# An involution's first block made of the image's edge rows, so that taps outside of the image are left out

## The chip, the cores and the metric

The kernel runs on one core of a Trainium2 chip. The metric is the device time of one launch in microseconds (us): the median of 3 runs for the kernel before. A core has a matrix engine (PE, or TensorE), which multiplies a stationary block of weights with a moving block and adds into PSUM; three elementwise engines, DVE (VectorE), ACT (ScalarE) and POOL (GpSimd); and SP, which here only issues DMA transfers. The engines run side by side and wait for each other through semaphores; each takes its own instructions in the order of the program.

## What is computed

The input `x` is 32 images of 256 channels and 32x32 pixels. Two residual layers follow each other; the change touches only the second, an *involution*: a 7x7 window over each pixel, with a window of weights that is computed for every pixel and shared by the 16 channels of each of 16 groups.

```python
# layer 0: x = x + conv3x3(groupnorm(x)), operands and result rounded to a 16-bit format, plus bias
x = x + L0(gn(x))
# layer 1, on v = gn(x):
y   = relu(bn(w1 @ v))                     # 256 -> 64 channels, 1x1
w   = (w2 @ y + b2).reshape(b, 16, 49, 32, 32)   # 49 weights per group and pixel
vp  = pad(v, 3 on each side)               # zeros outside of the image
out[b, g, c, h, j] = sum over (di, dj) in 7x7 of  w[b, g, (di,dj), h, j] * vp[b, g, c, h+di, j+dj]
x = x + out
```

`vp` is zero outside of the image. For the output row 0, the three taps `di` = 0, 1, 2 therefore give nothing; row 1 has two such taps and row 2 has one, and the same holds at the bottom for rows 31, 30 and 29. That is 12 of 32 x 7 = 224 pairs of a row and a vertical tap.

## The kernel before

An image is worked on in `NB` = 4 blocks of `BR` = 8 rows. A block takes four *stages*: the horizontal taps are split in two parts `v` (4 taps `dj`, then 3; one tap per 32 partitions, so 128 or 96 partitions), and the vertical taps in two parts `d` (`di` 0 to 3, then 4 to 6). An image has 16 stages, numbered here 0 to 15 in the order (k, v, d). A stage has two parts:

- `products`: weights times pixels, elementwise. DVE takes the first rows of the block, straight from PSUM; POOL takes the last rows, from an SBUF copy `ws` of the weights.
- `sums`: PE adds the products of all partitions into the 8 rows of the block. The stationary operand `shift` is a 0/1 matrix with 32 columns that moves a pixel by its `dj`. It fills only 32 of the array's 128 columns, so four such products stand side by side in four *column tiles*: tile `t` makes output rows 2t and 2t+1 (2 rows x 256 channels = 512 moving columns).

```python
COLS = (tuple(range(0, 4)), tuple(range(4, 7)))      # dj of v = 0 and 1
DI = ((0, 4), (4, 7))                                # di of d = 0 and 1
POOL_ROWS = (4, 6)                                   # POOL's first row, for d = 0 and 1

def load_pixels(b, i):                               # SBUF copy of the pixels, i = upper or lower half
    first = PAD1 if i == 0 else 0                    # 3 rows of zeros above, 16+3 rows of the image
    rows = XR - PAD1                                 # 19
    for r0, r1 in ((0, BR + PAD1), (BR + PAD1, rows)):
        for q in range(Q):                           # once per 32 partitions
            nc.sync.dma_start(xpix[i][q * W : (q + 1) * W, first + r0 : first + r1], ...)

def weights(b, k, v):                                # all 7 di at once, into PSUM
    for r in range(BR):
        for q, dj in enumerate(COLS[v]):
            nc.tensor.matmul(pw[q * W : (q + 1) * W, ...], y_pad[b % 2][:, k * BR + r, ...], w2_sb[:, dj, :], ...)
    nc.scalar.copy(ws[:p], pw[:p, 1, ...])           # rows 4 to 7, for POOL

def products(b, k, v, d, pw, ws):
    d0, d1 = DI[d]
    for r0, nr in ((0, 4), (4, 2), (6, 2)):
        on_pool = r0 >= (6 if (k, v) == (NB - 1, 1) else POOL_ROWS[d])
        tag, bufs = ("pg", 4) if on_pool else ("pa", 2) if nr == 4 else ("pb", 2)
        pt = prodp.tile([P, nr, d1 - d0, C], F32, tag=tag, name=tag, bufs=bufs)
        eng.tensor_tensor(o, win.unsqueeze(3).to_broadcast([p, nr, n, GC]), xin, ALU.mult)
        # ... prods[t] = the two rows of tile t

def sums(acc, v, d, prods):
    for i in range(d0, d1):
        for t in range(T):
            nc.tensor.matmul(acc[t * W : (t + 1) * W, :], shift[v][:p], prods[t][:p, :, i - d0, :], ...)

def finish(b, k, acc):                               # in three steps
    nc.scalar.copy(ob, acc...)                       # 1
    yield
    ... four nc.tensor.transpose(po[...], ob[...], ident)      # 2
    yield
    nc.vector.tensor_tensor(xt[:, :, cols], po..., xt[:, :, cols], ALU.add)   # 3: one add for 8 rows
    if k % 2 == 1:
        nc.sync.dma_start(out..., xt[:, :, cols])    # 16 rows

for n in range(FRONT, len(stages) + 3):              # one step per stage (cut to the order of issue)
    now = stages[n], products(*stages[n], *pws[n // 2])
    sums(acc, v, d, prods)                           # of stage n - 1
    next(ending, None)                               # a step of finish
    if n % 2 == 0:
        pws[n // 2 + 1] = weights(*stages[n + 2][:3])
    ... # one piece of the front of a later image
```

A *step* is one turn of this loop. In step n, DVE and POOL get the products of stage n, and PE gets the sums of stage n-1, on even steps the weights of stage n+2, and a piece of the *front* of a later image: group norm, the 3x3 convolution (`pc`, 18 matmuls for each of 4 units), the second group norm, the transposes `pt` and the product `py`. In step 0 the front has ACT apply the first group norm (`xq`), which the convolution's matmuls of step 1 read. In steps 1, 5, 9 and 13, POOL has an add (`x<-qb,x`) that waits for a convolution unit to have passed PE, DVE and ACT.

Of the kernel before, what the change touches and what calls it, by code (L numbers as in the profile page):

```python
# [9 lines left out]
F32 = mybir.dt.float32  # L10
AF = mybir.ActivationFunctionType
ALU = mybir.AluOpType

P = 128
B, C, H, W = 32, 256, 32, 32
N = H * W
NT = 512
RT = NT // W
CH = C // P
K0, PAD0 = 3, 1  # L20
H0 = H + 2 * PAD0
K1, PAD1 = 7, 3
TAPS = K1 * K1
CR = 64
G = 16
GC = C // G
# [7 lines left out]
Q = 4  # L34
COLS = (tuple(range(0, 4)), tuple(range(4, 7)))
DI = ((0, 4), (4, 7))
BR = 8
NB = H // BR
T = 4
HALF = H // 2  # L40
POOL_ROWS = (4, 6)
HOLD = 6
FRONT = -38
LOAD = -42
XR = HALF + 2 * PAD1


@with_exitstack
def tile_quant_conv_then_involution(
# [15 lines left out]
    nc = tc.nc  # L65
# [33 lines left out]
    pixels = {}  # L99
# [5 lines left out]
    for base, mult, step in ((0, 1, -GN), (GN - 1, -1, GN)):  # L105
        nc.gpsimd.affine_select(
            out=avg_g,
# [10 lines left out]
    shift = []  # L118
    for v, cols in enumerate(COLS):
        s = const.tile([P, W], F32, name=f"shift_{v}")  # L120
        nc.gpsimd.memset(s, 0.0)
        for q, dj in enumerate(cols):
            rows = s[q * W : (q + 1) * W]
            nc.gpsimd.affine_select(
                out=rows,
# [14 lines left out]
    nc.gpsimd.memset(three_halves, 1.5)  # L140

    xpix = [const.tile([P, XR, C], F32, name=f"xpix_{i}") for i in range(2)]
    nc.gpsimd.memset(xpix[0][:, :PAD1], 0.0)
    nc.gpsimd.memset(xpix[1][:, XR - PAD1 :], 0.0)
    y_pad = [const.tile([CR + 1, H, W + 2 * PAD1], F32, name=f"y_{i}") for i in range(2)]
    for t in y_pad:
        nc.gpsimd.memset(t[:CR], 0.0)
# [28 lines left out]
    prodp = ctx.enter_context(tc.tile_pool(name="prodp", bufs=2))  # L176
# [70 lines left out]
    def front(b):  # L247
# [65 lines left out]
        for r in range(0, H // 4, 2):  # L313
# [8 lines left out]
            for i in range(4):  # L322
                nc.sync.dma_start(xd[:, 4 * r + i : 4 * r + i + 5 : 4, :], xt4[i * W : (i + 1) * W])
            yield
        load_pixels(b, 0)

        py = ps_m.tile([P, NT], F32, tag="m", name="py")
# [18 lines left out]

    def load_pixels(b, i):

        first = PAD1 if i == 0 else 0
        rows = XR - PAD1  # L350
        for r0, r1 in ((0, BR + PAD1), (BR + PAD1, rows)):
            for q in range(Q):
                nc.sync.dma_start(
                    xpix[i][q * W : (q + 1) * W, first + r0 : first + r1],
                    pixels[b][:, i * (H - rows) + r0 : i * (H - rows) + r1, :],
                )

    def weights(b, k, v):


        pw = ps_w.tile([P, 2, NT], F32, tag="pw", name="pw")
        for r in range(BR):
            for q, dj in enumerate(COLS[v]):
                s = 2 * PAD1 - dj
                o = (r % 4) * K1 * G
                nc.tensor.matmul(  # L366
                    pw[q * W : (q + 1) * W, r // 4, o : o + K1 * G],
                    y_pad[b % 2][:, k * BR + r, s : s + W],
                    w2_sb[:, dj, :],
                    start=True,  # L370
                    stop=True,
                )
        p = W * len(COLS[v])
        ws = work.tile([P, 4, K1 * G], F32, tag="ws", name="ws")
        nc.scalar.copy(ws[:p], pw[:p, 1, : 4 * K1 * G].rearrange("p (r m) -> p r m", r=4))  # L375
        return pw, ws

    def products(b, k, v, d, pw, ws):

        d0, d1 = DI[d]  # L380
        p = W * len(COLS[v])
        n = (d1 - d0) * G
        half, first = divmod(k * BR, HALF)
        src = xpix[half]
        prods = {}
        for r0, nr in ((0, 4), (4, 2), (6, 2)):
            xin = bass.AP(
                tensor=src.tensor,
                offset=src[:p, first + r0 + d0, 0:1].offset,
                ap=[src[:p].ap[0], [C, nr], [GC, n], [1, GC]],  # L390
            )
            on_pool = r0 >= (6 if (k, v) == (NB - 1, 1) else POOL_ROWS[d])
            if on_pool:
                win = ws[:p, r0 - 4 : r0 - 4 + nr, d0 * G : d1 * G]
            else:
                o = (r0 % 4) * K1 * G
                win = pw[:p, r0 // 4, o : o + nr * K1 * G].rearrange("p (r m) -> p r m", r=nr)
                win = win[:, :, d0 * G : d1 * G]
            tag, bufs = ("pg", 4) if on_pool else ("pa", 2) if nr == 4 else ("pb", 2)
            pt = prodp.tile([P, nr, d1 - d0, C], F32, tag=tag, name=tag, bufs=bufs)  # L400
            o = pt[:p].rearrange("p r d (g c) -> p r (d g) c", c=GC)
            eng = nc.gpsimd if on_pool else nc.vector
            eng.tensor_tensor(o, win.unsqueeze(3).to_broadcast([p, nr, n, GC]), xin, ALU.mult)  # L403
            for t in range(r0 // 2, (r0 + nr) // 2):
                prods[t] = pt[:, 2 * t - r0 : 2 * t - r0 + 2]
        return prods

    def sums(acc, v, d, prods):
        d0, d1 = DI[d]
        p = W * len(COLS[v])  # L410
        for i in range(d0, d1):
            for t in range(T):
                nc.tensor.matmul(  # L413
                    acc[t * W : (t + 1) * W, :],
                    shift[v][:p],
                    prods[t][:p, :, i - d0, :],
                    start=v == 0 and i == 0,
                    stop=v == len(COLS) - 1 and i == K1 - 1,
                )

    def finish(b, k, acc):

        ob = work.tile([P, 2, C], F32, tag="ob", name="ob", bufs=1)
        nc.scalar.copy(ob, acc.rearrange("p (r c) -> p r c", c=C))  # L424
        yield
        po = acc.rearrange("p (h t r j) -> p h t r j", h=CH, t=T, r=2)
        for h in range(CH):
            for r in range(2):
                nc.tensor.transpose(po[:, h, :, r, :], ob[:, r, h * P : (h + 1) * P], ident)  # L429
        yield  # L430
        xt = x_tiles[b]
        cols = slice(k * BR * W, (k + 1) * BR * W)
        nc.vector.tensor_tensor(
            xt[:, :, cols], po.rearrange("p h t r j -> p h (t r j)"), xt[:, :, cols], ALU.add
        )
        if k % 2 == 1:
            cols = slice((k - 1) * BR * W, (k + 1) * BR * W)
            nc.sync.dma_start(out[b].rearrange("(h p) n -> p h n", p=P)[:, :, cols], xt[:, :, cols])
        if k == NB - 1:
            x_tiles.pop(b)  # L440
        yield
# [3 lines left out]
    stages = [  # L445
        (b, k, v, d) for b in range(B) for k in range(NB) for v in range(len(COLS)) for d in range(len(DI))
    ]
    per = len(stages) // B
    with tc.manual_schedule():
        fronts, done = {}, {}  # L450
        ending = iter(())
        acc = last = None
        pws = {}
        for n in range(FRONT, len(stages) + 3):
            if 0 <= n < len(stages):
                b, k, v, d = stages[n]
                now = stages[n], products(b, k, v, d, *pws[n // 2])
            else:
                now = None
            if last is not None:  # L460
                (b, k, v, d), prods = last
                if (v, d) == (0, 0):
                    acc = ps_acc.tile([P, NT], F32, tag="acc", name="acc")
                sums(acc, v, d, prods)
            next(ending, None)
            if last is not None and (v, d) == (len(COLS) - 1, len(DI) - 1):
                ending = finish(b, k, acc)
                next(ending)
            last = now
            b, at = divmod(n, per)  # L470
            if at == 0 and 0 <= b < B:
                load_pixels(b, 1)
            if 0 <= n + 2 < len(stages) and n % 2 == 0:
                pws.pop(n // 2 - 1, None)
                pws[n // 2 + 1] = weights(*stages[n + 2][:3])
            b, at = divmod(n - LOAD, per)
            if at == 0 and 0 < b < B:
                x_tiles[b] = load_x(b)
            b, at = divmod(n - FRONT, per)
# [48 lines left out]
```

## Time and profile before

| | before |
|---|---|
| time, median of 3 (lowest to highest) | 2862.68 us (2862.51 to 2863.04) |
| span of the profiled execution | 2862.9 us, granted PE clock 0.994 of full speed |
| busy: PE, DVE, POOL, ACT | 98%, 92%, 92%, 37% |
| DMA: mean share of the 16 engines, mean rate | 37.5% for all queues, 93 GB/s |
| matmul records on the sums' line | 14336 (7168 calls, two records each) |
| from the same point of one image to the next, in the middle of the run | 86.82 us (1483.47 to 1570.29) |

A profile row names the engine, the operation, the output and the inputs with their shapes (partitions x elements), and gives busy time, mean duration of one, and idle time before. Busy times of overlapping matmuls are not sums of their durations: four column tiles at work count once. The chain of waits is the list of work that, followed back from the last instruction, set the end: its pieces add up to the time.

### The profile page before, as it was taken

To read this page: it belongs to the slowest core of one execution; us is meant where nothing else is said; L and a number is where in the kernel's file an instruction comes from. 1 tells how busy PE (TensorE), PEld (TensorE's weight loads), DVE (VectorE), ACT (ScalarE), POOL (GpSimd) and SP (SyncE) were. 2 spreads that over 40 slices of the span, in tenths; PEclk is the share of its full clock that TensorE was granted. 3 is DMA by queue.
4 is the path that set the end of the run, shared out by engine and by line. 5 is a ranking of instruction groups with operands and counts; after the bars stand their busy time and mean duration, and the time that the engine had idled before them with its cause. 6 is when DMAs were issued, how large, how long until landed. Compare 5 with 4: busy or idle time off the path is not lost.

```text
span 2862.9 us, 73387 instructions
## 1 busy us (share of the span) xinstructions
PE 2805.4 (98%) x32576; PEld 1216.1 (42%) x32576; DVE 2621.2 (92%) x1131; ACT 1047.9 (37%) x2179; POOL 2639.3 (92%) x891
## 2 busy tenths in 40 slices
PE   5999999999999999999999999999999999999998
PEld 2444444444444444444444444444444444444443
DVE  1799999999999999999999999999999999999998
ACT  5443333333343433343433333333433333434210
POOL 2899999999999999999999999999999999999997
PEclk8999999999999999999999999999999999999999
DMA  2444433344433344332444333444333444323440
GB/s 94 98 105 114 93 81 98 83 108 101 101 87 83 97 109 93 97 98 72 106 111 94 83 98 82 107 104 101 84 87 94 108 93 100 95 73 90 97 101 16
DMA packets 93709, 267.45 MB, mean 93 GB/s; under 512 B 19341, under 2 KB 52109, under 8 KB 76750
## 3 DMA queue, kind: packets, MB, share of 16 engines
q1 hardware_dynamic: 93390, 262.75, 36.8%
q8 instruction: 254, 4.16, 0.6%
q14 instruction: 65, 0.53, 0.1%
HBM read 195.57 MB, written 67.11 MB: 92 GB/s over the span
## 4 chain that ended last, share of the span: by engine, by line
PE 91%; ACT 5%; issue 1%; POOL 1%; DVE 1%; DMA 1%; SPq 0%; ACTq 0%; POOLq 0%; DVEq 0%
PE acc L413 52%; PE pc L280 18%; PE pw L366 13%; PE pt L317 2%; PE py L330 2%; PE acc L429 2%; PE pg L196 1%; ACT xq L236 1%; POOL pg L403 1%; ACT qb L296 1%; ACT w L227 1%; DMA xpix<-xd 1%; DVE pb L403 1%; DVE pa L403 0%; ACT off L235 0%
## 5 line engine op out<-in xcount | busy, mean ns | idle before, releaser
L403 POOL TENSOR_TENSOR pg<-ws,xpix 128x2048 f32<-128x2048 f32 (+3 forms) x736 | 2469.2, 3387 | 69.5 <-ACT ws L375 52.7
L403 DVE TENSOR_TENSOR pa<-pw,xpix 128x4096 f32<-128x4096 f32 (+3 forms) x512 | 1987.1, 3882 | 162.2 <-ACT junk L188 87.2
L413 PE MATMUL acc<-pg,shift 128*32 128x512 f32 (+1 forms) x5376 | 1646.2, 596 | 1.4 <-POOL pg L403 1.3
L413 PE MATMUL acc<-pa,shift 128*32 128x512 f32 (+1 forms) x7168 | 1641.9, 596 | 2.6 <-DVE pa L403 2.4
L413 PE MATMUL acc<-pb,shift 96*32 96x512 f32 (+1 forms) x1792 | 825.9, 598 | 5.0 <-DVE pb L403 5.0
L413 PEld LDWEIGHTS acc<-pa,shift 128*32 128x32 f32 (+1 forms) x7168 | 374.2, 109 | 843.9 <-issue 792.7
L280 PE MATMUL pc<-xq,wq 128*128 128x512 f16 x2304 | 577.1, 387 | 18.6 <-ACT xq L236 15.3
L403 DVE TENSOR_TENSOR pb<-pw,xpix 128x1536 f32<-128x1536 f32 (+2 forms) x288 | 519.5, 1804 | 0.0
L366 PEld LDWEIGHTS pw<-w_sb,y 65*32 65x32 f32 x14336 | 414.2, 110 | 151.6 <-issue 150.5
L366 PE MATMUL pw<-w_sb,y 65*32 65x112 f32 x14336 | 446.0, 260 | 0.0
L375 ACT COPY ws<-pw 128x448 f32<-128x448 f32 (+1 forms) x256 | 135.8, 530 | 756.3 <-PE pw L366 750.3
L413 PEld LDWEIGHTS acc<-pg,shift 128*32 128x32 f32 (+1 forms) x5376 | 377.2, 109 | 64.8 <-issue 56.3
L280 PEld LDWEIGHTS <-wq 128*128 128x128 f16 x2304 | 213.5, 99 | 311.3 <-issue 120.1
L298 POOL TENSOR_TENSOR x<-qb,x 128x512 f32<-128x512 f32 x128 | 164.7, 1286 | 136.6 <-ACT qb L296 125.5
L424 ACT COPY ob<-acc 128x512 f32<-128x512 f32 x128 | 75.1, 587 | 481.8 <-PE acc L413 480.5
L413 PEld LDWEIGHTS acc<-pb,shift 96*32 96x32 f32 (+1 forms) x1792 | 174.1, 110 | 33.4 <-issue 18.0
L321 ACT COPY xt<-pt 128x512 f32<-128x512 f32 x128 | 75.0, 586 | 228.6 <-PE pt L317 127.4
L188 ACT ACTIVATE junk<-x 128x512 f16<-128x512 f32 (+1 forms) x192 | 148.0, 771 | 10.7 <-POOL x L298 6.1
L188 ACT ACTIVATE junk<-x,mean 128x1024 f16<-128x1024 f32 x128 | 147.2, 1150 | 4.1
L294 DVE TENSOR_SCALAR q<-pc 128x512 f16<-128x512 f32 x128 | 86.9, 679 | 31.6 <-PE pc L280 31.6
L429 PEld LDWEIGHTS acc<-ident,ob 128*128 128x128 f32 x512 | 53.6, 140 | 108.1 <-issue 82.2
L296 ACT ACTIVATE qb<-q,bias_sb 128x512 f32<-128x512 f16 x128 | 92.5, 722 | 12.0 <-DVE q L294 11.9
(52 smaller groups left out, 971.0 us busy)
## 6 DMA issues: line engine op xcount, KB each, us to landing
xpix<-xd SPq DMA_DIRECT2D x256, 352.0 KB, 6.5
xpix<-xd SPq DMA_DIRECT2D x256, 256.0 KB, 8.6
x<-in_x SPq DMA_DIRECT2D x64, 512.0 KB, 3.7
xd<-xt SPq DMA_DIRECT2D x512, 64.0 KB, 1.7
out<-x SPq DMA_DIRECT2D x64, 512.0 KB, 3.2
wf<-in_w SPq DMA_DIRECT2D x2, 1152.0 KB, 8.7
w_sb<-in_w SPq DMA_DIRECT2D x1, 199.1 KB
w_sb<-in_w SPq DMA_DIRECT2D x1, 64.0 KB, 9.7
```

Of the source, the lines that this page charges most:

```text
L188: nc.scalar.activation(junk[:, n0:n1], src[:, h, n0:n1], func, bias=bias, accum_out=self.sums[:, part, h : h + 1])
L280: nc.tensor.matmul(pc, wq[:, kh, k, mh * P : (mh + 1) * P], xq[:, kh, nt * RT + i0 : nt * RT + i0 + RT, j0 : j0 + W], start=n == 0, stop=n ...
L294: nc.vector.tensor_scalar(q, pc, F16_MAX, -F16_MAX, ALU.min, ALU.max)
L296: nc.scalar.activation(qb, q, AF.Identity, bias=bias_sb[:, mh : mh + 1])
L298: nc.gpsimd.tensor_tensor(xt[:, mh, cols], qb, xt[:, mh, cols], ALU.add)
L321: nc.scalar.copy(xt4, pt)
L366: nc.tensor.matmul(pw[q * W : (q + 1) * W, r // 4, o : o + K1 * G], y_pad[b % 2][:, k * BR + r, s : s + W], w2_sb[:, dj, :], start=True, s ...
L375: nc.scalar.copy(ws[:p], pw[:p, 1, : 4 * K1 * G].rearrange("p (r m) -> p r m", r=4))
L403: eng.tensor_tensor(o, win.unsqueeze(3).to_broadcast([p, nr, n, GC]), xin, ALU.mult)
L413: nc.tensor.matmul(acc[t * W : (t + 1) * W, :], shift[v][:p], prods[t][:p, :, i - d0, :], start=v == 0 and i == 0, stop=v == len(COLS) - 1 ...
L424: nc.scalar.copy(ob, acc.rearrange("p (r c) -> p r c", c=C))
L429: nc.tensor.transpose(po[:, h, :, r, :], ob[:, r, h * P : (h + 1) * P], ident)
```

## The change

Block 0 is no longer rows 0 to 7. It is rows 0 to 3 and 28 to 31; the other three blocks are rows 4 to 11, 12 to 19 and 20 to 27. All rows with taps outside of the image are then in one block, and in this block those products and sums are not made. The four column tiles of PE run side by side, so a tile gains time only if all four lose the same work; hence the pairs. Tile 0 takes rows 0 and 3 (3 + 0 taps outside), tile 1 rows 1 and 2 (2 + 1), tile 2 rows 28 and 31, and tile 3 rows 29 and 30: each pair leaves out 3 of 14.

In block 0, one stage of each `v` is "full": `di` 3 to 6 for the four upper rows and `di` 0 to 3 for the four lower rows, all inside of the image. The other is the "corner" stage: what is left, which is 6 row-taps at the top and 6 at the bottom, all made on DVE in six small instructions, and summed with matmuls of one row (256 columns) or two rows (512). Full and corner come in the order full, corner (v = 0), corner, full (v = 1).

```diff
+EDGE = BR // 2
+ROWS = [[*range(EDGE), *range(H - EDGE, H)]] + [
+    [*range(k * BR - EDGE, (k + 1) * BR - EDGE)] for k in range(1, NB)
+]
+HELD = ([*range(15), *range(25, H)], [*range(9, H - 1)])      # image rows in the two pixel buffers
-XR = HALF + 2 * PAD1
+XR = len(HELD[0])                                             # 22 rows, as before
-    nc.gpsimd.memset(xpix[0][:, :PAD1], 0.0)                  # rows of zeros are no longer needed
-    nc.gpsimd.memset(xpix[1][:, XR - PAD1 :], 0.0)
 def load_pixels(b, i):
-        for r0, r1 in ((0, BR + PAD1), (BR + PAD1, rows)):
+        for r0, r1 in (((0, 7), (15, 22), (7, 15)), ((0, 14), (14, 22)))[i]:
 def weights(b, k, v):
-                    y_pad[b % 2][:, k * BR + r, s : s + W],
+                    y_pad[b % 2][:, ROWS[k][r], s : s + W],
+    CORNERS = (                     # (column of pt, rows) to sum; (row, first di, last di + 1, where) to make
+        ([(0, 1), (1, 1), (2, 1)], [(3, 0, 3, slice(0, 3))]),
+        ([(3, 1), (4, 2)], [(2, 1, 3, slice(3, 6, 2)), (1, 2, 3, slice(4, 5))]),
+        ([(6, 0), (7, 0), (8, 0)], [(4, 4, 7, slice(6, 9))]),
+        ([(9, 2), (11, 0)], [(5, 4, 6, slice(9, 12, 2)), (6, 4, 5, slice(10, 11))]),
+    )
 def products(b, k, v, d, pw, ws):
+        if k == 0 and d == v:                                  # full
+            multiply(k, v, pw, ws, top, 0, 1, 4, 3, 7, False)  # DVE: 4 rows, di 3..6
+            for t in range(2, T):                              # POOL: rows 4 and 7, then 5 and 6, di 0..3
+                multiply(k, v, pw, ws, pt, 2 + t, 7 - 2 * t, 2, 0, 4, True)
+        elif k == 0:                                           # corner
+            for t, (moved, made) in enumerate(CORNERS):
+                for r, d0, d1, at in made:
+                    multiply(k, v, pw, ws, pt[:, at], r, 1, 1, d0, d1, False)
+        else:
-            on_pool = r0 >= (6 if (k, v) == (NB - 1, 1) else POOL_ROWS[d])
+                on_pool = r0 >= POOL_ROWS[d]
 def sums(acc, v, d, moves):
+        for i in range(most):
             for t in range(T):
+                if i < len(moves[t]):
+                    moving, of = moves[t][i]                   # of: 2 for both rows, else the row
+                    cols = slice(0, NT) if of == 2 else slice(of * C, (of + 1) * C)
+                    nc.tensor.matmul(acc[t * W : (t + 1) * W, cols], shift[v][:p], moving, ...)
 def finish(b, k, acc):
+        if k == 0:                                             # four adds of two rows, for the scattered rows
+            for t in range(2):
+                for r in range(2):
+                    nc.vector.tensor_tensor(at, po[:, :, t : t + 3 : 2, r], at, ALU.add)
-        if k % 2 == 1:                                         # out: 16 and 16 rows
+        for when, r0, r1 in ((NB - 2, 0, H - EDGE - BR), (NB - 1, H - EDGE - BR, H)):   # out: 20 and 12 rows
```

(Cut: the helper `multiply`, which holds the former body of `products`, the offsets of the rows in the pixel buffers, and the unchanged parts.)

Three things come along with the skipped taps. The two pixel buffers hold 22 rows of the image each, where they held 19 and 3 rows of zeros, so more is loaded. The exception by which DVE took more of stage 14 (k = 3, v = 1, d = 0: six rows in place of four) is gone, so POOL makes four rows there as in the other stages with d = 0. And the output leaves in 20 and 12 rows.

More of the change, by code (lines that the diff above doesn't have):

```diff
@@ L39 @@
 T = 4
-HALF = H // 2
+EDGE = BR // 2
[3 more added lines that the diff above has]
+HELD = ([*range(15), *range(25, H)], [*range(9, H - 1)])
+BASE = ((-PAD1, 15 - EDGE), (1, 1), (0, 0), (8, 8))
 POOL_ROWS = (4, 6)
@@ L347, in load_pixels @@
     def load_pixels(b, i):
-        first = PAD1 if i == 0 else 0
-        rows = XR - PAD1
-        for r0, r1 in ((0, BR + PAD1), (BR + PAD1, rows)):
+        for r0, r1 in (((0, 7), (15, 22), (7, 15)), ((0, 14), (14, 22)))[i]:
+            src = HELD[i][r0]
             for q in range(Q):
                 nc.sync.dma_start(
-                    xpix[i][q * W : (q + 1) * W, first + r0 : first + r1],
-                    pixels[b][:, i * (H - rows) + r0 : i * (H - rows) + r1, :],
+                    xpix[i][q * W : (q + 1) * W, r0:r1], pixels[b][:, src : src + r1 - r0, :]
                 )
@@ L376, in weights, with multiply @@
         return pw, ws
-    def products(b, k, v, d, pw, ws):
-        d0, d1 = DI[d]
+    def multiply(k, v, pw, ws, out, r0, step, nr, d0, d1, on_pool):
         p = W * len(COLS[v])
         n = (d1 - d0) * G
[L383 to L391, printed above, removed]
-            on_pool = r0 >= (6 if (k, v) == (NB - 1, 1) else POOL_ROWS[d])
[L393 to L406, printed above, removed]
@@ L408, in sums @@
-    def sums(acc, v, d, prods):
-        d0, d1 = DI[d]
-        p = W * len(COLS[v])
-        for i in range(d0, d1):
-            for t in range(T):
[L413 to L419, printed above, removed]
+        src = xpix[k // 2]
+        first = BASE[k][r0 // 4] + r0 + d0
@@ new lines, in multiply @@
+        xin = bass.AP(
+            tensor=src.tensor,
+            offset=src[:p, first, 0:1].offset,
+            ap=[src[:p].ap[0], [step * C, nr], [GC, n], [1, GC]],
+        )
+        rows = slice(r0 % 4, r0 % 4 + (nr - 1) * step + 1, step)
+        if on_pool:
+            win = ws[:p, rows, d0 * G : d1 * G]
+        else:
+            win = pw[:p, r0 // 4, : 4 * K1 * G].rearrange("p (r m) -> p r m", r=4)[:, rows, d0 * G : d1 * G]
+        if nr == 1:
+            win, xin = win[:, 0], xin[:, 0]
+            o = out[:p].rearrange("p d (g c) -> p d g c", c=GC)
+            win = win.rearrange("p (d g) -> p d g", g=G).unsqueeze(3).to_broadcast([p, d1 - d0, G, GC])
+            xin = xin.rearrange("p (d g) c -> p d g c", g=G)
+        else:
+            o = out[:p].rearrange("p r d (g c) -> p r (d g) c", c=GC)
+            win = win.unsqueeze(3).to_broadcast([p, nr, n, GC])
@@ new lines, in multiply, with products @@
+        eng = nc.gpsimd if on_pool else nc.vector
+        eng.tensor_tensor(o, win, xin, ALU.mult)
+    CORNERS = (
[3 more added lines that the diff above has]
+        ([(9, 2), (11, 0)], [(5, 4, 6, slice(9, 12, 2)), (6, 4, 5, slice(10, 11))]),
+    )
+    def products(b, k, v, d, pw, ws):
+        p = W * len(COLS[v])
+        moves = [[] for _ in range(T)]
+        if k == 0 and d == v:
+            top = prodp.tile([P, 4, 4, C], F32, tag="pa", name="pa")
+            multiply(k, v, pw, ws, top, 0, 1, 4, 3, 7, False)
+            for t in range(2):
+                moves[t] = [(top[:p, t : 4 - t : 3 - 2 * t, i], 2) for i in range(4)]
+            for t in range(2, T):
+                pt = prodp.tile([P, 2, 4, C], F32, tag="pg", name="pg", bufs=4)
+                multiply(k, v, pw, ws, pt, 2 + t, 7 - 2 * t, 2, 0, 4, True)
+                moves[t] = [(pt[:p, :, i], 2) for i in range(4)]
+        elif k == 0:
+            pt = prodp.tile([P, 12, C], F32, tag="pa", name="pa")
+            for t, (moved, made) in enumerate(CORNERS):
+                for r, d0, d1, at in made:
+                    multiply(k, v, pw, ws, pt[:, at], r, 1, 1, d0, d1, False)
+                moves[t] = [
+                    (pt[:p, at : at + 2] if of == 2 else pt[:p, at], of) for at, of in moved
+                ]
+        else:
+            d0, d1 = DI[d]
+            for r0, nr in ((0, 4), (4, 2), (6, 2)):
+                on_pool = r0 >= POOL_ROWS[d]
+                tag, bufs = ("pg", 4) if on_pool else ("pa", 2) if nr == 4 else ("pb", 2)
+                pt = prodp.tile([P, nr, d1 - d0, C], F32, tag=tag, name=tag, bufs=bufs)
+                multiply(k, v, pw, ws, pt, r0, 1, nr, d0, d1, on_pool)
+                for t in range(r0 // 2, (r0 + nr) // 2):
+                    moves[t] = [(pt[:p, 2 * t - r0 : 2 * t - r0 + 2, i], 2) for i in range(d1 - d0)]
+        return moves
@@ new lines, in sums @@
+    def sums(acc, v, d, moves):
+        p = W * len(COLS[v])
+        most = max(len(m) for m in moves)
+        for i in range(most):
+            for t in range(T):
+                if i < len(moves[t]):
+                    moving, of = moves[t][i]
+                    cols = slice(0, NT) if of == 2 else slice(of * C, (of + 1) * C)
+                    nc.tensor.matmul(
+                        acc[t * W : (t + 1) * W, cols],
+                        shift[v][:p],
+                        moving,
+                        start=(v, d, i) == (0, 0, 0),
+                        stop=(v, d, i) == (len(COLS) - 1, len(DI) - 1, len(moves[t]) - 1),
+                    )
@@ L425, in finish @@
         yield
-        po = acc.rearrange("p (h t r j) -> p h t r j", h=CH, t=T, r=2)
+        order = "p (h r t j) -> p h t r j" if k == 0 else "p (h t r j) -> p h t r j"
+        po = acc.rearrange(order, h=CH, t=T, r=2, j=W)
         for h in range(CH):
@@ L431, in finish @@
         xt = x_tiles[b]
[L432 to L435, printed above, removed]
-        if k % 2 == 1:
-            cols = slice((k - 1) * BR * W, (k + 1) * BR * W)
-            nc.sync.dma_start(out[b].rearrange("(h p) n -> p h n", p=P)[:, :, cols], xt[:, :, cols])
+        rows = xt.rearrange("p h (r j) -> p h r j", j=W)
+        if k == 0:
+            for t in range(2):
+                for r in range(2):
+                    first = ROWS[0][t if r == 0 else EDGE - 1 - t]
+                    at = rows[:, :, first : first + H - EDGE + 1 : H - EDGE]
+                    nc.vector.tensor_tensor(at, po[:, :, t : t + 3 : 2, r], at, ALU.add)
+        else:
+            at = rows[:, :, ROWS[k][0] : ROWS[k][-1] + 1].rearrange("p h r j -> p h (r j)")
+            nc.vector.tensor_tensor(at, acc.rearrange("p (h n) -> p h n", h=CH), at, ALU.add)
+        for when, r0, r1 in ((NB - 2, 0, H - EDGE - BR), (NB - 1, H - EDGE - BR, H)):
+            if k == when:
+                cols = slice(r0 * W, r1 * W)
+                nc.sync.dma_start(
+                    out[b].rearrange("(h p) n -> p h n", p=P)[:, :, cols], xt[:, :, cols]
+                )
         if k == NB - 1:
```

## The prediction

> **What bounds the kernel now.** I read the page's busy shares first, then the chain of waits over one image in the middle of the run, then the timelines of POOL and DVE over the same image. The shares alone don't decide:
>
> ```profile
> PE 2805.4 (98%) x32576; PEld 1216.1 (42%) x32576; DVE 2621.2 (92%) x1131; ACT 1047.9 (37%) x2179; POOL 2639.3 (92%) x891
> ...
> PE 91%; ACT 5%; issue 1%; POOL 1%; DVE 1%; DMA 1%; SPq 0%; ACTq 0%; POOLq 0%; DVEq 0%
> ```
>
> PE is at 98%, but two other engines at 92% could be hard behind it. The chain from 1475 to 1590 us (start, length, what) shows how steps 0 to 5 go together:
>
> ```profile
> 1479.20 2.71 PE acc L413 x24
> 1481.91 1.56 PE pw L366 x48
> ...
> 1486.33 1.26 ACT xq L236
> 1487.58 0.04 issue
> 1487.62 1.48 PE pc L280 x6
> 1489.10 2.71 PE acc L413 x24
> 1491.82 1.53 PE pw L366 x64
> 1493.35 0.98 PE pc L280 x4
> 1494.33 3.57 PE acc L413 x32
> 1497.90 0.54 PE pg L196 x4
> 1498.44 1.79 PE pc L280 x8
> 1500.23 2.71 PE acc L413 x24
> 1502.94 1.53 PE pw L366 x48
> ```
>
> See that PE follows PE without a gap. The one stretch that the chain gives to ACT, 1483.5 to 1487.6, hides PE's sums of stage 0 (a four-tap stage, 3.57) and the four transposes of the block before (0.59 elsewhere in this chain): 4.16 us of work in a stretch of 4.15. So the 5% of ACT are no idle time of PE. Where an image starts (step 1, 1483.47) this repeats at 1570.29: 86.82 us an image, nearly all of it PE. Four taps cost 3.57 and three cost 2.71, so one tap of two rows costs 0.86, and 0.13 belongs to the stage.
>
> Next, how close POOL and DVE are. From POOL's timeline:
>
> ```profile
> 1484.78 1.29 POOL L298 TENSOR_TENSOR x<-qb,x 128x512 f32<-128x512 f32 x1 [1.17 <-ACT qb L296]
> 1486.03 20.19 POOL L403 TENSOR_TENSOR pg<-ws,xpix 96x2048 f32<-96x2048 f32 x6
> 1506.17 1.30 POOL L298 TENSOR_TENSOR x<-qb,x 128x512 f32<-128x512 f32 x1
> 1507.41 20.20 POOL L403 TENSOR_TENSOR pg<-ws,xpix 96x2048 f32<-96x2048 f32 x6
> ```
>
> The second number is a stretch of back-to-back instructions: POOL doesn't rest from 1484.78 to 1527.6. The first two products of the first stretch (2 x 3.67 from start to start) are those of stage 2 and end at 1493.4; PE wants them at 1494.33. POOL is 1 us ahead, no more. PE is the bound, and POOL would be next.
>
> [...] the sums' matmuls start in groups of four within 0.02 us, and the next four come 0.43 us later, though one matmul's record lasts 596 ns. No run yet shows tiles with unequal matmuls, on which the corner stages rest. [...] eight f16 matmuls of 512 columns take 1.79 us (224 ns each), and the f32 sums take twice that per record. [...] Here the 4096- and 1536-element products take 4417 and 1745 ns, so 1.044 ns an element and 142 ns fixed[...]. [...] the 4096-element form keeps to 4.41 or 4.42 us with POOL busy beside it.
>
> **The change part by part.**
> 1. *Sums, removed (on the path).* In block 0 a tile gets per `v` four taps of 512 columns and 768 columns more in the corner: 2816 in place of 7 x 512 = 3584. The missing 768 are 1.5 taps: 1.5 x 0.86 = 1.29 us, twice an image: 2.58. A corner stage comes to 0.13 + 1.5 x 0.86 = 1.42. All four tiles have 768, in the order 256, 256, 256 for tiles 0 and 2, 256, 512 for tile 1, and 512, 256 for tile 3. Over 32 images: 82.6 us, which is also 3/14 of a quarter of the sums.
> 2. *Products on POOL (beside PE).* Block 0 loses both 1536-element instructions: 2 x 2.815 = 5.63. Stage 14 gets one of 2048 back: 3.69. Net -1.94 of 82.12 busy per image.
> 3. *Products on DVE (beside PE).* Before, 4.417 + 3.347 + 1.745 = 9.51 per `v`. After, 4.417 for the full stage and 3072 elements in six instructions: 3.21 + 6 x 0.142 = 4.06; together 8.48. Twice 1.03 is 2.07 saved. Stage 14 saves its 2.28. The four adds of 128 elements cost 4 x (142 + 134) = 1.10 in place of 0.68. Net -3.9 of 81.8.
> 4. *Loads.* 22 rows in place of 19: the pixel loads grow by 22/19, from 159 to 185 MB (by the page's issue sizes), so the DMA share goes from 37% to about 40%. The lower half has eight steps of time, the upper six; before the first image a transfer or two is added, about 1 us either way. The two memsets that go (0.74 each) lay in the opening.
> 5. *Weights, convolution, norms, transposes:* the same.
>
> Steps 2 and 3 must now fit the new timing, because two short steps follow each other. I walk it, with zero at the start of step 1. PE: sums of stage 0 and transposes 4.15, pc 1.48: 5.63. Step 2: corner 1.42, pw 1.53, pc 0.98: 9.56. Step 3: corner 1.42, pg 0.54, pc 1.79: 13.3. Step 4: full 3.57 and pw 1.53: 18.4, then pg 0.31. Step 5 wants stage 4 at 18.7; step 7 wants stage 6 at 29.9.
> - POOL: the add ends at 2.6 as before (it hangs on step 0). Stage 3's two products: 9.9, wanted at 13.3. Stage 4's need `ws`, ready at about 9.3: they end at 17.3, wanted at 18.7. Stage 5: 20.1; the add: 21.4; stage 6: 28.8, wanted at 29.9. The same 1.1 to 1.4 us ahead as before.
> - POOL at the end of an image, in the times of before: after the add at 1552.1, stage 14 ends at 1559.5 (wanted at 1560.6), 15 at 1562.3 (wanted 1566.0), the next stage 0 at 1569.6 (wanted 1570.3). This is the tightest place: 0.7 us.
> - DVE: corner 1 ends at about 2.5 (wanted at 5.6); corner 2 waits until its buffer is free at 3.6 and ends at 7.3; the add of the block before, then stage 3: 12.2, wanted at 13.3. Stage 4, from 12.2: 16.6, wanted at 18.7.
>
> Nothing arrives late, so the PE saving should show in full. The last image has no front beside it, so DVE sets its pace (82 us of work in 87); it saves 2 to 4 us there, the same size. Sum: 2862.7 - 82.6 = 2780.
>
> **The rivals.**
> (a) *POOL becomes the bound.* For: 92% busy, 1 us ahead, and given one product more in stage 14. Against: it has 1.94 us less per image. If the 0.7 us at the turn of the image is eaten and each image loses 0.5 to 1 us, 16 to 32 us come back: 2796 to 2812.
> (b) *Unequal tiles don't run free.* Each call is two records, so if every row of four had to wait for its longest, a corner would cost 1 + 1 + 0.5 = 2.5 taps (512, 512 and 256 columns for i = 0, 1, 2) in place of 1.5; one tap too much in 64 corners is 55 us, result 2835. Half of that, if the rows partly overlap: 2807. For: no trace shows it. Against: [...] fixed costs per record are small (the 112-column weights: 64 records in 1.53 us, 24 ns each).
> (c) *DVE or ACT cannot follow two short steps.* For: six small instructions and 1.1 us ahead of stage 3; ACT's group-norm sums must be ready 2.6 us earlier relative to step 1. Against: ACT is 37% busy, and its sums before step 3 end at 1494.6, that is 11.1 us after the zero of the walk, though they wait for the weights' copy, which itself comes 1.3 us earlier now; PE asks at 11.0. Cost if it fails: some tenths an image, 10 us.
> (d) *More comes off than PE's share.* PE has no other idle time to give: at most the 2 to 4 us of the last image. 2775.
>
> **Range and chances.** The centre 2780 takes the PE saving in full. (d) gives the low end 2768 with some slack for the opening; (a) and (c) together, at half their size, give the high end 2802. The 2% line is at 2805.4, 26 us above the centre: it needs (b), or (a) at nearly full size. I give (b) 5% and a heavy (a) 5%. Faster by over 2%: 0.90; within 2%: 0.08; slower by over 2%: 0.02.
>
> **What would show it.** In the chain, corner stages as PE acc pieces of about 1.42 us, with full ones at 3.57, and an image at 84.2 us. If corners measure 1.8 or more, (b) holds. If waits of the sums on POOL's `pg` grow from 8 us (6.5 and 1.3 in the list of waits) to tens, (a). POOL should have some 80.2 us busy per image and DVE 77.9. The DVE products of one row should lie on 142 + 1.044 n ns. The prediction is wrong if PE shows gaps at steps 2 to 5, or if the corner's columns don't cost what 512-column ones do.

## The result and the profile after

| | before | changed |
|---|---|---|
| time, median (lowest to highest) | 2862.81 us (2862.51 to 2863.04) | 2784.56 us (2783.0 to 2785.68) |
| ratio, 95% interval | | 0.9726 (0.9709 to 0.9743): 78.3 us or 2.7% off |
| one image in the middle of the run | 86.82 us | 84.25 us |
| busy in such an image: PE, DVE, POOL | 86.66, 81.76, 82.12 us | 84.09, 77.30, 80.17 us |
| matmul records on the sums' line | 14336 | 14080 |

From the page of the changed kernel, the busy shares and the chain by engine:

```profile
PE 2721.5 (98%) x32320; PEld 1222.7 (44%) x32320; DVE 2478.3 (89%) x1451; ACT 1048.0 (38%) x2179; POOL 2576.7 (93%) x857
...
PE 90%; ACT 4%; issue 2%; POOL 2%; DMA 1%; DVE 1%; POOLq 0%; SPq 0%; ACTq 0%; DVEq 0%
```

All three busy engines lost work, but the shares moved in different directions: PE stays at 98%, DVE falls to 89%, and POOL, which lost least, rises to 93% of a shorter span. The chain of the changed kernel in steps 1 to 5 of one image (start, length, what):

```profile
1445.01 1.48 PE pc L287 x6
1446.49 1.43 PE acc L462 x16
1447.92 1.54 PE pw L371 x51
1449.45 0.98 PE pc L287 x4
1450.44 1.43 PE acc L462 x16
1451.86 0.54 PE pg L203 x4
1452.40 1.79 PE pc L287 x8
1454.19 3.57 PE acc L462 x32
1457.76 1.53 PE pw L371 x48
1459.29 0.31 PE pg L203 x2
1459.60 3.57 PE acc L462 x32
```

The two corner stages take 1.43 us each, where the kernel before had 2.71 and 3.57 in these two places and 2.71 instead of the 3.57 at 1454.19. PE follows PE without a gap, as before. What the walk of the prediction feared, a late product in the two short steps, isn't there: stage 4's sums begin at 1459.60, 14.6 us after the 1445.01, and the walk had 18.7 - 4.15 = 14.6.

The 28 images from the second to the twenty-ninth each take 84.25 us from their last transposes to the next image's; before, 86.82. That is 2.57 x 28 = 72.0 of the 79.6 us between the two profiled spans. The start (up to the last transposes of the first image) gives 4.1 and the last three images with what follows 3.6. The last three took 86.56, 80.52 and 75.26 us before, and 83.69, 79.96 and 75.42 now.

### The profile page after: what moved, and what is told of

Same layout as the page of the kernel before. It is cut to its first block, busy times and chain, and to the rows that moved or that the text cites. A ratio compares the mean times of both kernels' runs of the same rounds, so it can differ in the third digit from the quotient of the medians.

```text
span 2783.3 us, 73320 instructions
## 1 busy us (share of the span) xinstructions
PE 2721.5 (98%) x32320; PEld 1222.7 (44%) x32320; DVE 2478.3 (89%) x1451; ACT 1048.0 (38%) x2179; POOL 2576.7 (93%) x857
## 2 busy tenths in 40 slices
DMA packets 99853, 292.60 MB, mean 105 GB/s; under 512 B 21389, under 2 KB 62349, under 8 KB 86990
## 3 DMA queue, kind: packets, MB, share of 16 engines
q1 hardware_dynamic: 99534, 287.93, 42.5%
## 4 chain that ended last, share of the span: by engine, by line
PE 90%; ACT 4%; issue 2%; POOL 2%; DMA 1%; DVE 1%; POOLq 0%; SPq 0%; ACTq 0%; DVEq 0%
PE acc L462 50%; PE pc L287 18%; PE pw L371 13%; PE pt L324 2%; PE py L337 2%; PE acc L479 2%; POOL pg L408 2%; PE pg L203 1%; ACT xq L243 1%; ACT qb L303 1%; ACT w L234 1%; DMA xpix<-xd 0%; DVE pa L408 0%; ACT u L236 0%; ACT off L242 0%
## 5 line engine op out<-in xcount | busy, mean ns | idle before, releaser
L408 POOL TENSOR_TENSOR pg<-ws,xpix 96x2048 f32<-96x2048 f32 (+2 forms) x704 | 2407.0, 3451 | 23.5 <-PE acc L462 17.6
L408 DVE TENSOR_TENSOR pa<-pw,xpix 128x4096 f32<-128x4096 f32 (+7 forms) x832 | 2006.2, 2446 | 223.1 <-ACT junk L195 86.9
L462 PE MATMUL acc<-pa,shift 128*32 128x512 f32 (+3 forms) x7680 | 1566.2, 570 | 6.9 <-DVE pa L408 6.8
L462 PE MATMUL acc<-pg,shift 128*32 128x512 f32 (+1 forms) x5248 | 1481.5, 599 | 6.3 <-POOL pg L408 6.3
L287 PE MATMUL pc<-xq,wq 128*128 128x512 f16 x2304 | 576.8, 387 | 18.7 <-ACT xq L243 15.5
L462 PE MATMUL acc<-pb,shift 128*32 128x512 f32 (+1 forms) x1152 | 531.1, 597 | 0.8 <-DVE pb L408 0.8
L462 PEld LDWEIGHTS acc<-pg,shift 128*32 128x32 f32 (+1 forms) x5248 | 354.9, 110 | 65.2 <-issue 51.2
L408 DVE TENSOR_TENSOR pb<-pw,xpix 128x1536 f32<-128x1536 f32 x192 | 335.0, 1745 | 0.0
L195 ACT ACTIVATE junk<-x 128x512 f16<-128x512 f32 (+1 forms) x192 | 147.9, 770 | 10.7 <-POOL x L305 6.2
L462 PEld LDWEIGHTS acc<-pb,shift 128*32 128x32 f32 (+1 forms) x1152 | 111.2, 109 | 8.5 <-issue 4.3
```

The lines of the kernel that those rows point to most:

```text
L195: nc.scalar.activation(junk[:, n0:n1], src[:, h, n0:n1], func, bias=bias, accum_out=self.sums[:, part, h : h + 1])
L287: nc.tensor.matmul(pc, wq[:, kh, k, mh * P : (mh + 1) * P], xq[:, kh, nt * RT + i0 : nt * RT + i0 + RT, j0 : j0 + W], start=n == 0, stop=n ...
L408: eng.tensor_tensor(o, win, xin, ALU.mult)
L462: nc.tensor.matmul(acc[t * W : (t + 1) * W, cols], shift[v][:p], moving, start=(v, d, i) == (0, 0, 0), stop=(v, d, i) == (len(COLS) - 1, l ...
```

## Experiments

All are edits of the changed kernel. Images are given as in the table, in the middle of the run, where they repeat to some 0.3 us.

**1. Pairs of adjacent rows.** The skipped taps and the products stay the same; only the rows of a column tile differ.

```diff
-    moves[t] = [(top[:p, t : 4 - t : 3 - 2 * t, i], 2) for i in range(4)]      # rows 0 and 3, 1 and 2
+    moves[t] = [(top[:p, 2 * t : 2 * t + 2, i], 2) for i in range(4)]          # rows 0 and 1, 2 and 3
-    multiply(k, v, pw, ws, pt, 2 + t, 7 - 2 * t, 2, 0, 4, True)
+    multiply(k, v, pw, ws, pt, 2 * t, 1, 2, 0, 4, True)
     # and CORNERS and the rows of the four adds for these pairs: 1, 5, 5 and 1 row-taps in the
     # four tiles, in place of 3 each
```

> The same taps are left out, but each column tile takes two adjacent rows (0 and 1, 2 and 3, 28 and 29, 30 and 31), so the corner stage has 256 columns in tiles 0 and 3 and 1280 in tiles 1 and 2, where the changed kernel has 768 in each. Work on DVE, POOL and DMA is the same. Theory (PE's longest tile sets a corner): a corner takes 0.13 + 2.5 x 0.86 = 2.28 us in place of 1.43, so 0.86 x 64 = 55 us come back: 2840 us. Rival (the sum of columns over the four tiles counts, or the gain is DVE's and POOL's): no difference from 2784.6 us.

2830.36 us (2828.53 to 2830.7), ratio to before 0.9883 (0.9868 to 0.9898). An image takes 85.95 us, 1.70 more than the changed kernel, where 2 x 0.86 = 1.72 was expected. The chain around the first corner:

```profile
1472.01 1.48 PE pc L287 x6
1473.49 1.11 PE acc L462 x7
1474.61 0.10 PE pw L371
1474.70 0.04 issue
1474.74 0.72 PE acc L462 x3
1475.46 0.10 PE pw L371 x3
1475.57 0.20 PE acc L462 x2
1475.77 1.53 PE pw L371 x58
```

From 1473.49 to 1475.77 are 2.28 us, the expected length to the digit. Inside of it, weights' matmuls (`pw`) turn up in the chain from 1474.61 on, while the long tiles still sum until 1475.77: the next work begins beside them, but the stage is no shorter for it. So the longest tile sets a stage, here 2.28 us against 1.43 with the same columns in all four, and the pairing is worth two thirds of the gain in an image (1.70 of 2.57). The total came back by 45.8 and not by 55 us, because 1.70 holds for the middle of the run, while the last three images took 235.3 us here and 239.1 in the changed kernel; experiment 5 takes that up.

**2. Corner sums at the old width.** Each tile sums three times 512 columns in a corner.

```diff
-                moves[t] = [(pt[:p, at : at + 2] if of == 2 else pt[:p, at], of) for at, of in moved]
+                moves[t] = [(pt[:p, 2 * i : 2 * i + 2], 2) for i in range(3)]
```

> Only PE's part of the change is undone: each tile of a corner gets three matmuls of 512 columns, as before the change, over arbitrary products of the stage (the block's sums are then not the reference's). DVE and POOL keep their lighter work. Theory (PE's columns carry the gain): a corner takes 2.71 us, 82 us come back, about 2866 us, an image 86.8 us. Rival (lighter DVE and POOL carry a part of it): between 2785 and 2850 us, by that part.

2855.66 us (2855.05 to 2855.88), ratio 0.9973 (0.9962 to 0.9984). Busy times in one image (us; PE, its weight loads, DVE, ACT, POOL, then the granted clock, the DMA share and GB/s):

```profile
1485.26:1572.08 86.82, 86.66 (x1018) 37.94 (x1018) 77.59 (x46) 32.62 (x69) 80.27 (x27) 1.00 0.43 105
```

The image is back at 86.82 us, the value before the change to the last digit, with DVE 4.2 and POOL 1.9 us lighter than before. In the middle of the run the gain is PE's columns and nothing else. What remains is at the two ends: of the 8.7 us between the two profiled spans, 2.3 lie in the opening and 6.8 in the last three images (235.6 against 242.3), and 0.4 are lost after them.

**3. POOL's two products put back,** unread.

```diff
         elif k == 0:
+            idle = prodp.tile([P, 2, 3, C], F32, tag="pg", name="pg", bufs=4)
+            multiply(k, v, pw, ws, idle, 6, 1, 2, 0, 3, True)
```

> POOL gets its two removed products of block 0 back (1536 elements in each corner stage, which nobody reads); all else is as changed. POOL then has 80.2 + 5.6 = 85.8 us of work an image against 84.25 of PE. Theory (PE bounds the changed kernel, POOL a few per cent behind): POOL becomes the bound, an image takes 86 to 87 us, 2840 to 2875 us, with the sums waiting for pg. Rival (POOL has slack enough): 2784.6 us.

2850.75 us (2849.07 to 2852.31), ratio 0.9956 (0.9939 to 0.9972). One image, and POOL's timeline through it:

```profile
1449.50:1535.86 86.36, 85.25 (x1012) 39.41 (x1011) 77.41 (x46) 32.61 (x68) 85.58 (x29) 1.00 0.43 105
```

```profile
1479.07 20.18 POOL L408 TENSOR_TENSOR pg<-ws,xpix 96x1536 f32<-96x1536 f32 x6
1499.21 1.27 POOL L305 TENSOR_TENSOR x<-qb,x 128x512 f32<-128x512 f32 x1
1500.45 20.17 POOL L408 TENSOR_TENSOR pg<-ws,xpix 96x2048 f32<-96x2048 f32 x6
1520.59 1.28 POOL L305 TENSOR_TENSOR x<-qb,x 128x512 f32<-128x512 f32 x1
```

POOL is busy for 85.58 of 86.36 us, and the waits of the sums for `pg` went from 20.3 us (14.0 + 6.3) in the whole changed kernel to 113.8 (77.2 + 36.6). Two instructions of 2.8 us cost 2.11 us an image, 66 us in all. So the changed kernel keeps its gain only because the same taps left POOL as well. The run says this of the new split of stage 14, which gives POOL 3.69 us more. With the old split and its two products kept, POOL would have the 82.12 us of before, under PE's 84.25; that was not tried. As an engine that merely lies beside the path POOL is worth nothing (experiment 2), as the next bound it is worth four fifths of the change (2.11 of 2.57).

**4. The skip carried on to the weights.**

```diff
+                row = ROWS[k][r]
+                m0, m1 = G * max(0, PAD1 - row), G * min(K1, H + PAD1 - row)
                 nc.tensor.matmul(
-                    pw[q * W : (q + 1) * W, r // 4, o : o + K1 * G], ..., w2_sb[:, dj, :],
+                    pw[q * W : (q + 1) * W, r // 4, o + m0 : o + m1], ..., w2_sb[:, dj, m0:m1],
-        nc.scalar.copy(ws[:p], pw[:p, 1, ...])
+        m = 4 * G if k == 0 else K1 * G
+        nc.scalar.copy(ws[:p, :, :m], pw[:p, 1, ...][:, :, :m])
```

> The skip is carried on to the weights: in block 0 the weights' matmuls make only the taps inside of the image, 704 columns in place of 896 over the eight rows, and ACT copies only the four taps that POOL reads. Theory (PE bounds, and its time goes with columns down to 64): 0.33 us off each of two weight groups an image, 21 us in all: 2763 us. Rival (a record of 64 columns costs as much as one of 112, because its weight load of 110 ns or its issue sets it): no difference, 2784.6 us.

2759.05 us (2757.04 to 2760.66), ratio 0.9635 (0.9621 to 0.965). The chain has the two weight groups of block 0 at

```profile
1498.85 1.22 PE pw L373 x64
...
1509.21 1.21 PE pw L373 x48
```

1.22 and 1.21 us in place of 1.53, by the columns (704/896 of 1.53 is 1.20), so a group with records of 64 to 112 columns still goes by their length, though their weight loads take 110 ns as before. An image takes 83.46 us, 0.79 less. The 0.15 or so beyond the two groups fit PE's small wait of 0.16 us for `xq`, which is gone from 29 images (15.5 to 10.7 us in the whole run): ACT's copy of the weights got shorter by 0.16 (0.53 to 0.37) just ahead of `xq`. That last step is read from the lists of waits, not tried by itself.

**5. PE kept busy in two waits of the last image.** The tail of the changed kernel's chain shows why:

```profile
2706.75 1.36 PE acc L462 x16
2708.11 0.03 DVEq L408
2708.14 2.94 DVE pa L408
2711.09 0.04 issue
2711.13 6.53 PE acc L462 x32
...
2768.31 9.53 PE acc L462 x50
```

A four-tap stage (x32) takes 6.53 us here, and 3.57 elsewhere. The last image has no front beside its sums, so PE waits for DVE or POOL; the granted clock is halved, from 1.00 to 0.50 of full speed, from 2710.2 for 6.8 us, and again from 2768.2 for 6.8 us. The kernel before has one such stretch in its last two images, at the very end (from 2847.2 for 6.8 us), where its chain has

```profile
2847.78 9.30 PE acc L413 x52
```

```diff
+            for at, count in ((3, 12), (14, 24)):            # steps of the last image
+                if n == len(stages) - per + at:
+                    idle = ps_c.tile([P, NT], F32, tag="pc", name="pc")
+                    for i in range(count):
+                        nc.tensor.matmul(idle, wq[:, 0, 0, :P], xq[:, 0, :RT, :W], ...)   # unused
```

> The changed kernel, with PE kept busy in two waits of the last image, by 12 matmuls of 512 columns (2.6 us, result unused) before the sums of its stage 3 and 24 (5.2 us) before those of stage 14. There PE waits for DVE and POOL, and in the changed kernel's trace its granted clock is halved from 2710.2 and from 2768.2 us for 6.8 us each: 32 records take 6.53 us in place of 3.57, and the last 50 take 9.53 where another run with a full clock shows 6.21. Theory (the 4 us that the change falls short by are lost there, to the clock after a wait): some 6 us off, 2778 us. Rival (the last image is set by DVE and POOL alone): no difference, 2784.6 us.

2780.64 us (2779.8 to 2781.66), 3.9 less than the changed kernel; the highest run lies below the lowest of the changed kernel. The chain of the same places:

```profile
2709.97 3.64 PE acc L462 x32
...
2761.11 5.29 PE pc L546 x24
2766.39 6.19 PE acc L462 x56
```

The clock stays at 1.00 in both places, 6.53 became 3.64, and the last image takes 71.33 us, not 75.42. So 4.1 us of the last image were the clock after a wait and not the work of DVE and POOL. Of the expected 6 us two thirds came: the clock is not all that the end waits for.

**6. The exception of stage 14 put back.**

```diff
-                on_pool = r0 >= POOL_ROWS[d]
+                on_pool = r0 >= (6 if (k, v) == (NB - 1, 1) else POOL_ROWS[d])
```

> Only the exception of stage 14 is put back: DVE makes six rows there and POOL two. POOL then has 76.5 us an image and DVE 79.6, both under PE's 84.25. Theory (PE bounds every stage): an image stays at 84.25 us, the time within 3 us of 2784.6. Rival (POOL's 0.7 us before the turn of the image is too little, so the exception helps): up to 10 us faster.

2782.85 us (2782.66 to 2783.02), ratio 0.972 (0.9707 to 0.9733); an image takes 84.25 us. Moving 3.69 us from POOL and 2.28 to DVE in each image changes nothing in the middle of the run. The 1.7 us less lie at the end, where the clock has its part too (from 2711 to 2717 its mean is 0.72, against 0.50 in the changed kernel, and the sums behind the wait take 5.34 us and not 6.53); they are not explained further.

**7. The best version:** the edits of 4 and 5 together.

> The skipped weights (2759 us) and the two fillings together. Theory of the clock: the low clock around 2688 us of that run's trace goes, 2 to 4 us, so about 2756 us. Rival: 2759 us.

2756.56 us (2755.75 to 2757.74), ratio to before 0.9629 (0.9616 to 0.9642), 2.5 us under experiment 4, though the ranges of the two overlap. This is the fastest kernel of the study, by 28.0 us against the change. Experiment 4 has a low clock around 2688 us (a mean of 0.78 from 2685.3 to 2690.3), which was expected to go. The mean clock of the whole run rose from 0.992 there to 0.994 here, but the gain is not shown to come from the fillings: the last image, which holds the fillings, takes 71.31 us against 70.90 in experiment 4. What got shorter is the image before it (80.80 to 77.85), with no filling ahead of it.

**8. Another order in block 0:** full, corner, full, corner.

```diff
-        if k == 0 and d == v:
+        if k == 0 and d == 0:
```

> Only the order within block 0 is changed: full, corner, full, corner in place of full, corner, corner, full. PE has the same work. By the walk, POOL's add ends at 2.6, and stage 2's two products then end at 9.9 to 10.0, where PE wants them at 9.56 (with two corners in a row POOL has until 13.3). Theory (POOL is 1 us behind PE, and the order gives it its time): some 0.4 us an image, 13 us slower, about 2797 us. Rival (the order doesn't matter): 2784.6 us.

2792.37 us (2791.95 to 2793.08), ratio 0.9753 (0.974 to 0.9767). An image takes 84.67 us, 0.42 more, as the walk had it. In the chain, stage 2's sums are the ones that got longer:

```profile
1454.20 1.53 PE pw L371 x64
1455.73 0.98 PE pc L287 x4
1456.72 3.98 PE acc L462 x26
1460.70 0.54 PE pg L203 x4
```

3.98 in place of 3.57. The wait hides well: PE is not idle, since three tiles start at 1456.65 and go on every 0.43 us while tile 3 waits for its product until 1457.11, and the list of waits shows only 16.9 + 3.2 us for `pg` against 14.0 + 6.3 in the changed kernel. It shows in the length of the stage. In the total, 7.8 us came and not 13, because this run's last three images (234.3 us) are again shorter than the changed kernel's.

## Why the prediction was right

It said 2780 us (2768 to 2802); 2784.56 were measured.

- *Bound.* PE sets an image, as said: gapless chain, and experiment 2 brings back 86.82 when PE's columns alone come back.
- *Step 1, sums on the path.* 2.58 us an image and 1.42 a corner were predicted; 2.57 and 1.43 were measured. The premise that no run had shown, unequal matmuls in four tiles that run free of each other, holds: a tile takes the sum of its own columns (1.43 with 256 and 512 mixed), a stage the longest tile (experiment 1). Rival (b) is out.
- *Step 2, POOL.* -1.94 us an image predicted, -1.95 measured (82.12 to 80.17). Rival (a), POOL as the bound, was one step away: 5.6 us of work more and it is true (experiment 3). Its sign, the waits of the sums for `pg`, did grow, from 7.8 to 20.3 us, but 17.1 of these lie in the last two images and none between 200 and 2600 us. The prediction gave 0.7 us as the tightest place; experiment 6 shows that it sufficed.
- *Step 3, DVE.* The short products take 948, 678 and 411 ns for 768, 512 and 256 elements; 142 + 1.044 n gives 944, 676 and 409. The total fell by 4.46 us an image and not by 3.9: six small instructions overlap at their ends and take 3.67 us together, where their durations add up to 4.07. Beside the path this changed nothing. Rival (c) is out: no gap in steps 2 to 5.
- *Step 4, loads.* The transfers carry 292.60 MB in all, against 267.45, as worked out (22/19 of the pixels' part), and the share is 42.5% on the main queue, where "about 40%" was said. The chain doesn't see them in the middle of the run.
- *The step that was off: the ends.* "It saves 2 to 4 us there", the prediction says of the last image: it saved -0.16, and the one before it 0.55. The term had been read from DVE's busy time alone. In its place stand PE's waits and its clock. In the last two images PE waits for POOL as well as for DVE (the 17.1 us above; 7.2 with POOL's share of stage 14 taken back, experiment 6, where those for DVE grow from 22.3 to 34.1). And the clock is halved there, to 0.50, three times for 6.8 us each, from 2631.7, 2710.2 and 2768.2, where the kernel before had it at 0.50 for 6.8 us once. With the last two filled (experiment 5; the very last is one that the kernel before has as well) the last image takes 71.33 us, 3.9 less than before. The first was not tried by itself. The last image but one takes 77.9 us in experiments 2, 7 and 8, and 79.6 to 80.0 in the changed kernel and in experiments 1, 5 and 6. That the clock makes this difference was the author's estimate and is not shown: the mean clocks of the whole runs, 0.993 to 0.995 and 0.991 to 0.994, overlap, and their work differs too.
- *The opening* went the other way: 4.1 us saved, 1.5 beyond the one image in it. There POOL is not yet ahead (in the chain before, the sums of stage 2 wait for `pg` from 97.7 to 105.1 us), so the corner stages, which need no POOL, save its time on the path: from the first sums to the first transposes it is 21.7 us (93.4 to 115.1) in place of 25.4 (93.8 to 119.2). The memsets that are gone lie before that, where only 0.4 us come off. The ends and the opening together leave 3.0 of the predicted 82.6 us out between the profiled spans, and 4.3 between the medians; the two partly cancel, so the total came nearer than its parts. Rival (d), more than PE's share, holds for the opening and not for the total.

## What to carry to other kernels

Work that was skipped in some of PE's tiles paid only as far as the longest tile got shorter (experiment 1: 0.87 in place of 2.57 us an image for the same skipped taps). So lay the skipped pieces out so that all parts lose the same. The gain was then the columns taken off times the measured time of a column, to 1% (2.57 us, 2.58 predicted). Before counting on it, ask how far the next engine is behind, and take work off it with the same skip; a step order that lets that engine have two short steps in a row was worth 0.42 us an image. And look for the same useless taps upstream: their weights were still being made, and leaving them out gave another 25 us.

## What was not expected of the hardware

- PE's clock fell in a wait of only 3.0 us (2708.11 to 2711.13): from 2710.2 on, 2.1 us into the wait, it was at 0.50 for 6.8 us, and the sums behind the wait took 6.53 us in place of 3.57. In experiment 5, with the wait filled, they took 3.64 at a clock of 1.00. So a wait of 3 us near the end cost another 3.
- The low stretches near the end differ between the kernels: the last two images hold three of 6.8 us in the changed kernel and one in the kernel before. What decides which wait is followed by a low clock is not shown. The last three images took 232.5 to 242.5 us over the runs of this study, and not in the order of their work: 239.1 in the changed kernel, and 235.6 in experiment 2, where PE has more to do. A difference of a few us is therefore safer read from the middle of the run, where an image repeats to some 0.3 us, than from the totals.
